# Graph attention, two layers: the first superchunk of layer 1 is gathered before the last rows of its table are there

## The chip, the cores and the metric

The kernel runs on one core of one Trainium2 chip. The metric is the device time of one execution in microseconds (us). The engines are PE (matmul, with PEld for its weight loads), DVE (vector), ACT (scalar), POOL (here the engine that issues the gathers) and SP (which issues nearly all other DMAs). Each has an instruction queue of its own that it works off in order; between queues only semaphores hold an order.

## The reference

Two graph attention layers over 6250 nodes with 256 features and 200,000 edges that are sorted by destination; layer 0 has four heads, layer 1 has one. Cut to one layer:

```python
hx = (x @ Wg).reshape(n, h, f)
te = relu(edge_attr @ We + be) * exp(x @ Wo + bo)[src][:, None]
s2, d2, ea2 = _add_self_loops(src, dst, te, n)   # a loop has the mean of its node's te
he = (ea2 @ Wge).reshape(-1, h, f)
al = leaky_relu((hx * a_s).sum(-1)[s2] + (hx * a_d).sum(-1)[d2] + (he * a_e).sum(-1), 0.2)
al = softmax of al over the edges of each destination
out = segment_sum(hx[s2] * al[:, :, None], d2) + b
```

Ahead of it stand a layer norm and a relu; layer 0's output goes through a relu with its residual and is layer 1's input. For each edge the row `hx[src]` is needed, with a few numbers that hang on the same node. Layer 1's row of a node can be computed only when layer 0 has finished that node.

## The kernel before, in words

**Tiles.** The edges are cut into columns of 128 edges, and the columns into superchunks of C = 24 (3072 edges). There are 66 superchunks a layer (`NS`): 64 with 24 columns, then one with 14 and one with 13. Step k counts superchunks over both layers: k = 0 to 65 are layer 0, 66 to 131 are layer 1. Since edges are sorted by destination, a superchunk holds all edges of some 95 neighbouring nodes, its window, which starts at node `base[s]` and is at most M = 112 nodes long.

**Tables.** `T[0]` and `T[1]` lie in device memory, one row of 268 or 260 floats for each node: the node's `hx`, its parts of the logit, and the exponential for its edges. `gather` issues one indirect DMA for each column on POOL; it fetches 128 rows of `T[l]` by the source indices `src` into `G`, one of three buffers (`gp[k % 3]`) of 128 x 24 x 270 floats.

**A superchunk's steps.** `spread`, `parts`, `blocks` bring the destination's part of the logit to the edges (DVE, a little PE). `rphase1` and `rphase2` compute the edge part (PE, ACT), `adst` adds the destination's part on PE, `edge_rows` transposes the result (DVE), `onehots` makes S, the matrices that say which of the window's nodes each edge belongs to. `logits`, `ends`, `links`, `maxima` need G: logits, running maxima per node, and the exponentials. `scale` multiplies G with them (on DVE in layer 0, on ACT in layer 1), `carried` adds what the superchunk before left of a shared node, `sums` multiplies S with G on PE and adds all columns in PSUM, `evict` copies the sums out.

**Finishing nodes.** `finish` merges a window's sums with its self loops and makes the node's new features. In layer 0 three row steps follow. `rows1` transposes the features (PE, then ACT), `rows2` multiplies them with layer 1's weights (PE), `rows3` adds the bias into a staging row (`t1row`, two buffers by the superchunk's parity), takes an exponential on ACT and stores it with three DMAs on SP: to `T[1]`, to the window copies `nd` (two arrays), and one number to the neighbouring window. In layer 1 only `rows3` does something: it stores the output.

**The order.** It is written out by hand: the program's text is the order of each engine's queue, and the framework adds the semaphore waits, for device memory too. `edges` loops over the superchunks, gathers one ahead, and finishes a window one or two steps later. The last three superchunks of a layer, called a, b, c (k = 63, 64, 65 and again 129, 130, 131), are interleaved by hand in `ending`, with `pv` and `late` the two before them (62 and 61). `after` is the first superchunk of layer 1 (k = 66), or None in the second layer. At the end of `ending` stood the gather of `after`, behind the last `rows3`, then its other steps up to `onehots`. The loop then goes on with the gather of 67.

`flag` and `general` are a slow way for inputs that fit no window; `checks` adds up what would call for it.

Of the kernel before, what the change touches and what calls it, by code (L numbers as in the profile page):

```python
# [22 lines left out]
F32 = mybir.dt.float32  # L23
# [8 lines left out]
P = 128  # L32
# [47 lines left out]
class Kernel:  # L80
# [364 lines left out]
    def indices(self, wp):  # L445
# [82 lines left out]
        self.slink = cp.tile([1, NS], F32, name="slink")  # L528
        V.tensor_tensor(self.slink, sc0[0:1, 0, :], sc0[0:1, 2, :], op=OP.is_equal)
        self.direct = max(NS - 2, 0)  # L530
        yield

        qd31 = cp.tile([1, 4, NS], F32, name="qd31")
# [9 lines left out]
    def checks(self, qd31, low):  # L543

        cp, V, NS, N, base, ll = self.cp, self.nc.vector, self.NS, self.N, self.base_f, self.lastloc
        chk = cp.tile([1, 9, NS + 1], F32, name="chk")
        V.memset(chk, 0.0)
        V.tensor_scalar(chk[:, 0, :NS], ll[0:1, :], float(M - 1), None, op0=OP.is_gt)
        V.tensor_scalar(chk[:, 5:9, :NS], qd31, 31.0, None, op0=OP.is_gt)
        nb = cp.tile([1, NS + 1], F32, name="nb")  # L550
        V.tensor_copy(nb[:, :NS], base[0:1, :])
        yield
        V.memset(nb[:, NS:], float(N))
        V.tensor_sub(nb[:, :NS], nb[:, 1:], nb[:, :NS])
        V.tensor_scalar(chk[:, 1, :NS], nb[:, :NS], float(M), None, op0=OP.is_gt)
        V.tensor_scalar(chk[:, 2, :NS], nb[:, :NS], 1.0, None, op0=OP.is_lt)
        yield
        V.tensor_copy(chk[:, 3, :NS], low)
        if self.direct:
            V.tensor_scalar(chk[:, 4, :self.direct], base[0:1, :self.direct], float(N - M), None, op0=OP.is_gt)  # L560
        V.memset(self.bad[:, 0:1], 0.0)
        V.tensor_reduce(self.bad[0:1, 0:1], chk.rearrange("p a b -> p (a b)"), axis=AX.X, op=OP.add)
        yield
# [80 lines left out]
    def edges(self, ctx):  # L644
        nc = self.nc
        self.gp += [self.pool(f"gath{i}", 1, ctx) for i in range(1, 3)]
        self.sp = self.pool("onehot", 2, ctx)
        self.wp = self.pool("work", 2, ctx)
        self.np_ = self.pool("nodes", 2, ctx)
        self.xp = self.pool("index", 1, ctx)  # L650
        self.ps_y = self.pool("ps_y", 1, ctx, space=PSUM)
        self.ps_1 = self.pool("ps_1", 1, ctx, space=PSUM)
        self.ps_f = self.pool("ps_f", 1, ctx, space=PSUM)
        self.lf = self.ps_1.tile([P, 512], F32, name="lf")
        nc.vector.memset(self.lf[0:4, 0:1], -BIG)
# [12 lines left out]
        self.adst(steps[0])  # L668
        self.onehots(steps[0])
        drain(self.soon)  # L670
        self.edge_rows(steps[0])

        pv = late = None
        self.ahead, self.rest = 1, None
        for k, st in enumerate(steps):
            nx = steps[k + 1] if k + 1 < len(steps) else None
            if st["s"] + 2 >= self.NS:
                continue
            for q in steps[k + 1:k + 3]:
                if q["L"] is st["L"] and "tw" not in q:  # L680
                    self.nodes(q)
            self.load_lb(k + 2)
            left = 99
            if self.ahead < len(self.groups):
                left = self.groups[self.ahead][0] - 2 - (self.ahead + 2 >= len(self.groups)) - k
            if self.rest is None and left <= 2:
                gi = self.index_load(self.ahead, self.xp)
                self.rest = self.index_group(self.ahead, self.xp, gi)
            if st["s"] + 3 == self.NS:
                self.ending(st, *steps[k + 1:k + 3], pv, late, steps[k + 3] if k + 3 < len(steps) else None)  # L690
                pv = late = None
# [12 lines left out]
            self.load_fl(k + 1)  # L704
            self.blocks(nx)
            drain(self.maxima(st))
            drain(y)
            self.load_ea(k + 2)
            self.rphase2(nx)
            self.adst(nx)  # L710
            if "S" not in st:
                self.onehots(st)
            if st["rows"]:
                self.scale_rows(st)
            else:
                drain(self.scale(st))
            self.carried(st)
            self.sums(st)
            if late:
                self.rows3(late)  # L720
                late = None
            self.onehots(nx)
            if pv:
                drain(self.finish(pv))
            self.evict(st)
            if pv:
                self.rows1(pv)
                late = pv
            self.index_on(left)
            if k >= 6:  # L730
                next(self.late, None)
                next(self.late, None)
            self.edge_rows(nx)
            if st["s"] + 4 == self.NS:
                drain(self.finish(st))
            pv = st
        self.flag()
# [9 lines left out]
    def ending(self, a, b, c, pv, late, after):  # L747
# [42 lines left out]
        drain(self.maxima(b))  # L790
        self.evict(a)
        n = b["C"]
# [71 lines left out]

    def flag(self):
        nc = self.nc
# [8 lines left out]
    def gather(self, st):  # L875
        nc, L = self.nc, st["L"]
        st["G"] = G = self.G0 if st["k"] == 0 else self.gp[st["k"] % 3].tile([P, C, 270], F32, name="G")
        idx = self.src[:, st["o"]:st["o"] + st["C"]]
        last = st["C"] - 1
        for c in (range(0) if st["k"] == 0 and self.CX > last else (last, *range(last))):  # L880
            nc.gpsimd.indirect_dma_start(  # L881
                out=G[:, c, 0:L.TW], out_offset=None, in_=self.T[L.l][0:self.N, :],
                in_offset=bass.IndirectOffsetOnAxis(ap=idx[:, c:c + 1], axis=0))
# [109 lines left out]
    def spread(self, st):  # L993


        if "Q" in st:
            return
        V = self.nc.vector
        q = self.pair(st["k"]) or [st]
        if len(q) < 2 or q[0]["C"] != q[1]["C"]:  # L1000
            q = [st]
        i, n, s = len(q), 32 * st["C"], st["s"]
        lb = st["lb2"] if i > 1 else st["lb"].unsqueeze(1)
        Q = self.wp.tile([P, 2, P], BF, name="Q")
        V.tensor_tensor(lb[:, :, :n], lb[:, :, :n], self.k_part.unsqueeze(2).to_broadcast([P, i, n]), op=OP.is_equal)  # L1005
        V.tensor_tensor(Q[:, :i].rearrange("p i (k j) -> p (i k) j", j=32),
                        self.k_32.unsqueeze(1).to_broadcast([P, 4 * i, 32]),
                        self.qsel[:, s:s + i, :].rearrange("p i k -> p (i k)").unsqueeze(2)
                        .to_broadcast([P, 4 * i, 32]), op=OP.is_equal)
        for j, t in enumerate(q):  # L1010
            t["Q"] = Q[:, j, :]

    def onehots(self, st, c0=0, c1=C):
        nc, o = self.nc, st["o"]
# [557 lines left out]
```

## Time and profile before

| what | value |
|---|---|
| median of 3 runs | 4052.73 us (4050.89 to 4054.78) |
| the profiled execution | 4055.1 us, its span 4053.3 us |
| busy: PE, DVE, ACT, POOL | 65%, 60%, 28%, 74% of the span |
| mean granted PE clock | 0.779 of full speed |
| gathers on POOL | 3102 + 24 in the prologue |

Times in timelines are microseconds from the start of the span: start, duration, engine, line, operation, output and inputs, how many instructions were merged, and in brackets how long the engine sat idle before and what released it. "issue" means that nothing the profile shows was waited for. In a list of waits the columns are the total in us, the times, and the longest. In tables of windows each engine has its busy time and number of instructions, then come the granted clock of PE (1.00 is full speed), the busy share of the 16 DMA engines, and GB/s. A matmul in float32 is shown as two instructions, so 24 matmuls are x48. An engine with a q behind its name is that engine's DMA queue, or its sequencer.

### The profile page before, as it was taken

The numbers are of one execution on the slowest core, as the hardware profiler recorded it, in microseconds if no ns is written. First come the engines' busy times: TensorE is split into PE (matmuls) and PEld (weight loads), VectorE is DVE, ScalarE is ACT, GpSimd is POOL, SyncE is SP. The second block draws the span as 40 slices with busy tenths as digits, with TensorE's granted clock in tenths as the row PEclk, the third lists the DMA queues.
The fourth block names the chain that finished last, engine by engine and source line by source line (L and its number), as shares of the span: only waits on it lengthen the run. The fifth ranks groups of instructions, "written<-read, shape, count | busy, mean of one in ns | idle before, by whom it ended". The sixth has DMA issues, their size and how long they took to land.

```text
span 4053.3 us, 37237 instructions
## 1 busy us (share of the span) xinstructions
PE 2639.2 (65%) x9878; PEld 1719.8 (42%) x9878; DVE 2436.3 (60%) x6063; ACT 1117.1 (28%) x2670; POOL 2998.9 (74%) x3253
## 2 busy tenths in 40 slices
PE   8776766666666766766646656656656566566565
PEld 6454444444444444444433433434434334334343
DVE  7887877877877877877744434333344343343445
ACT  5211111111111111111123434434334344343341
POOL 5777777777777777777747777777777777777775
PEclk9888878888887888888777777777777777777777
DMA  7455555555555555555534455455445445445443
GB/s 246 135 158 143 150 155 144 150 154 146 149 154 149 147 152 151 146 151 153 138 108 134 136 143 142 131 142 141 134 139 141 135 138 144 132 138 143 134 136 96
DMA packets 239250, 583.15 MB, mean 144 GB/s; under 512 B 64235, under 2 KB 96401, under 8 KB 238971
## 3 DMA queue, kind: packets, MB, share of 16 engines
q0 software_dynamic: 150144, 422.75, 39.3%
q1 hardware_dynamic: 88477, 157.30, 12.1%
q8 instruction: 85, 1.39, 0.1%
q14 instruction: 128, 1.05, 0.1%
q10 hardware_dynamic: 416, 0.67, 0.1%
HBM read 542.72 MB, written 37.86 MB: 143 GB/s over the span
## 4 chain that ended last, share of the span: by engine, by line
POOL 33%; DVE 27%; issue 14%; ACT 9%; PE 9%; DMA 8%; DVEq 0%; SPq 0%; ACTq 0%; POOLq 0%
POOL G L881 33%; DVE G L1192 8%; DMA G<-T,src 7%; ACT G L1201 7%; PE y L981 4%; DVE S L1021 4%; PE u L1211 2%; DVE lb L1005 2%; PE ps L439 1%; DVE m L1140 1%; DVE rt L1070 1%; ACT R L982 1%; DVE al L1088 1%; DVE al L1086 1%; DVE fb L1101 1%
## 5 line engine op out<-in xcount | busy, mean ns | idle before, releaser
L881 POOL DMA_INDIRECT G<-T,src x3102 | 2946.7, 950 | 1003.3 <-issue 916.3
L1211 PE MATMUL u<-G,S 128*128 128x270 f32 (+1 forms) x6252 | 1569.1, 414 | 187.4 <-DVE G L1182 184.1
L1211 PEld LDWEIGHTS u<-G,S 128*128 128x128 f32 x6252 | 1279.1, 206 | 479.0 <-DVE G L1182 212.2
L1201 ACT ACTIVATE G<-G,kw 128x256 f32<-128x256 f32 x1512 | 609.0, 497 | 0.0
L982 ACT ACTIVATE R<-y,webd 128x1024 f32<-128x1024 f32 (+2 forms) x264 | 235.4, 892 | 1322.8 <-PE y L981 817.4
L1108 PE MATMUL lf<-ident,fb 128*36 128x128 f32 (+1 forms) x132 | 50.3, 381 | 821.3 <-DVE fb L1101 795.7
L1084 DVE TENSOR_TENSOR G<-rt,G 128x96 f32<-128x96 f32 (+1 forms) x132 | 30.3, 230 | 866.0 <-DMA G<-T,src 866.0
L1192 DVE TENSOR_TENSOR G<-G,kps 128x6144 f32<-128x6144 f32 (+3 forms) x77 | 440.9, 5734 | 0.0
L1021 DVE TENSOR_TENSOR S<-kps,loc 128x3072 f32<-128x3072 f32 x132 | 437.6, 3315 | 4.6
L981 PE MATMUL y<-ea,webd 64*128 64x256 f32 (+1 forms) x1056 | 393.7, 840 | 50.9 <-ACT R L982 50.9
L990 PE MATMUL zad<-R,wea 128*64 128x384 f32 (+1 forms) x1056 | 308.2, 726 | 158.5 <-ACT R L982 158.2
L1108 PEld LDWEIGHTS lf<-ident,fb 128*36 128x36 f32 (+1 forms) x132 | 15.8, 119 | 863.4 <-DVE fb L1101 837.0
L990 PEld LDWEIGHTS zad<-R,wea 128*64 128x64 f32 x1056 | 88.2, 189 | 428.3 <-ACT R L982 339.8
L1216 ACT ACTIVATE U<-u 128x270 f32<-128x270 f32 (+1 forms) x132 | 51.8, 393 | 631.0 <-PE u L1211 631.0
L1243 DVE SCALAR_TENSOR_TENSOR mg<-U,mw 128x1 f32<-128x1 f32 x66 | 14.5, 220 | 281.3 <-ACT mw L1241 281.3
L981 PEld LDWEIGHTS y<-ea,webd 64*128 64x128 f32 x1056 | 124.7, 289 | 123.7 <-ACT R L982 70.3
L1174 DVE SCALAR_TENSOR_TENSOR G<-U,kw,G 1x257 f32<-1x257 f32 x62 | 29.6, 478 | 185.1 <-ACT G L1201 185.1
L1070 DVE STREAM_TRANSPOSE rt<-zad 128x768 f32<-128x768 f32 (+1 forms) x130 | 126.1, 970 | 8.5 <-PE zad L1056 8.5
L1042 PE MATMUL zad<-a,Q 128*128 128x12 bf16 (+1 forms) x132 | 26.1, 197 | 156.6 <-DVE a L1037 156.2
L439 PE MATMUL fin<-wg,h1T 128*128 128x260 f32 x264 | 125.3, 623 | 3.7 <-ACT h1T L1306 3.7
L1005 DVE TENSOR_TENSOR lb<-lb,kps 128x1536 bf16<-128x1536 bf16 (+1 forms) x68 | 112.9, 1661 | 0.0
L1316 ACT ACTIVATE t1row<-t1row 128x1 f32<-128x1 f32 x66 | 13.4, 203 | 349.9 <-DVE t1row L443 349.9
(195 smaller groups left out, 2238.4 us busy)
## 6 DMA issues: line engine op xcount, KB each, us to landing
G<-T,src POOLq DMA_INDIRECT x3102, 2.8
ea<-in_ea_dram SPq DMA_DIRECT2D x64, 768.0 KB
lb<-locrow SPq DMA_DIRECT2D x64, 384.0 KB
nd<-t1row SPq DMA_DIRECT2D x66, 225.8 KB
tw<-nd SPq DMA_DIRECT2D x66, 225.8 KB
tw<-T SPq DMA_DIRECT2D x66, 117.2 KB
T<-t1row SPq DMA_DIRECT2D x66, 113.8 KB
tw<-in_x_dram SPq DMA_DIRECT2D x66, 112.0 KB
```

The lines of the kernel that those rows point to most:

```text
L439: self.nc.tensor.matmul(ps[:, :L.MW], hT[:, k, :], self.wg[L.l][:, k, :], start=(k == 0), stop=(k == 1))
L881: nc.gpsimd.indirect_dma_start(out=G[:, c, 0:L.TW], out_offset=None, in_=self.T[L.l][0:self.N, :], in_offset=bass.IndirectOffsetOnAxis(ap= ...
L981: nc.tensor.matmul(y[:, i, :n], self.webd[l][r, :], ea[r, w], start=True, stop=True)
L982: nc.scalar.activation(R[:, :, w], y[:, :, :n], AF.Relu, bias=self.be[l])
L990: nc.tensor.matmul(st["zad"][i * PH:(i + 1) * PH, o], self.wea[l][0], R[:, i, w], start=True, stop=False)
L1005: V.tensor_tensor(lb[:, :, :n], lb[:, :, :n], self.k_part.unsqueeze(2).to_broadcast([P, i, n]), op=OP.is_equal)
L1021: nc.vector.tensor_tensor(st["S"][:, c0:c1, :], self.k_iota.unsqueeze(1).to_broadcast(w), self.loc[:, o + c0:o + c1].unsqueeze(2).to_broad ...
L1070: V.transpose(rv[:, :32 * c].rearrange("p (b n) -> p b n", b=2), z.rearrange("p (b n) -> p b n", b=2)[:, :, :16 * c])
L1108: self.nc.tensor.transpose(self.lf[0:e.shape[1], 1:P + 1], e, self.ident)
L1192: nc.vector.tensor_tensor(v, v, pw[:, c0:c1, :].unsqueeze(3) .to_broadcast([P, c1 - c0, H, L.F]), op=OP.mult)
L1201: self.nc.scalar.activation(v, v, AF.Copy, scale=st["w"][:, c:c + 1])
L1211: nc.tensor.matmul(st["u"][:, :L.W], S[:, i, :], G[:, i, 0:L.W], start=(j == 0), stop=(j == c - 1))
```

## The change

**The gather of `after`** is issued between the last of a's sums and `evict(a)`, into a's own buffer `G` (no new buffer is taken), columns in order from 0. By then the table holds the rows of all nodes ahead of a's first, so rows of nodes from `base[NS - 3]` on are fetched as what stands there. The steps of the two windows before are put further up for that: `rows3(late)`, `rows1(pv)`, `rows2(pv)` and `rows3(pv)` are all issued ahead of the gather. This order holds in both layers' endings, as the function is the same.

**What is added in layer 0's step 4** (`lacking`): two DMAs put zeros into the table's last 256 rows (a row read early is multiplied with 0 later, so it must be finite), and a few DVE instructions make `known`, which is 1 for each edge of superchunk 66 whose source lies ahead of the first missing node and 0 otherwise, and `k_lack`, the node number of each of the last 256 rows, or -1 where the row isn't missing.

**The completion.** `sources` loads the 3072 source indices of 66 into all 128 partitions (1.57 MB), into c's buffer, once c's sums are done. After c's `rows3`, `lack_rows` loads the table's last 256 rows as two tiles, `select` makes two one-hot matrices (a missing node's row against 3072 edges; one lies in c's buffer beside the indices, the other in an S buffer), and `complete` does for each column two matmuls, one-hot times rows, and on DVE `G = G * known + product`. Its 24 columns go in three groups of 8, between `blocks`, `rphase2` and `adst`, and behind `edge_rows` and `onehots`. The products use three places in turn: the two halves of the PSUM tile `y`, and `fin`. On the reference's inputs the first missing node is 6048, and 95 of the 3072 edges have a missing source. A new check sends inputs whose first missing node is below 6250 - 256 to the general way.

```diff
@@ checks
+        if self.early:
+            V.tensor_scalar(chk[:, 4, NS:], base[0:1, NS - 3:NS - 2], float(N - 2 * P), None, op0=OP.is_lt)
@@ edges
+            if k == 4 and self.early:
+                self.lacking()
@@ ending
         drain(self.maxima(a))
+        self.rows3(late)
         drain(y)
         self.load_ea(k + 2)
         self.rphase2(b)
         self.adst(b)
+        self.rows1(pv)
         drain(self.scale(a))
         self.carried(a)
         n = a["C"]
+        self.rows2(pv)
         self.sums(a, (0, n // 3))
-        self.rows3(late)
+        self.rows3(pv)
         self.edge_rows(b)
...
-        self.rows1(pv)
         self.spread(c)
         self.parts(c)
         self.sums(a, (n // 3, n // 2))
         self.links(b)
         self.sums(a, (n // 2, n))
+        early = after and self.early
+        if early:
+            self.gather(after, a["G"])
         self.load_fl(k + 2)
-        self.rows2(pv)
         drain(self.maxima(b))
...
         self.adst(c)
-        self.rows3(pv)
         self.carried(b)
...
         self.sums(c, (1, m), (0, 1))
+        if early:
+            self.sources(after)
         f = self.finish(b)
...
         if after:
-            self.gather(after)
+            fill = iter(())
+            if early:
+                self.lack_rows(after)
+                self.select(after)
+                fill = self.complete(after)
+            else:
+                self.gather(after)
             self.nodes(after)
             self.spread(after)
             self.parts(after)
             self.blocks(after)
+            for _ in range(C // 3):
+                next(fill, None)
             self.rphase2(after)
             self.adst(after)
+            for _ in range(C // 3):
+                next(fill, None)
             self.edge_rows(after)
             self.onehots(after)
+            drain(fill)
@@ new functions
+    def lacking(self):
+        nc, cp, N, NS = self.nc, self.cp, self.N, self.NS
+        V, W = nc.vector, self.L[1].TW
+        none = self.a["x"][N:N + 2 * P, :].rearrange("n d -> (n d)")[0:P * W].rearrange("(p w) -> p w", w=W)
+        for n in (N - 2 * P, N - P):
+            nc.sync.dma_start(self.T[1][n:n + P, :], none)
+        first = self.base_f[:, NS - 3:NS - 2]
+        self.known = cp.tile([P, C], F32, name="known")
+        V.tensor_scalar(self.known, self.src[:, 0:C], first, None, op0=OP.is_lt)
...
+    def sources(self, st):
+        n = C * P
+        X = self.gp[2].tile([P, C, 270], F32, name="G").rearrange("p c d -> p (c d)")
+        st["row"] = r = X[:, 0:n].bitcast(I32)
+        self.nc.sync.dma_start(r, self.a["srow"].rearrange("c p -> (c p)").partition_broadcast(P))
+        st["sel"] = [self.sp.tile([P, C, P], F32, name="S").rearrange("p c e -> p (c e)"), X[:, n:2 * n]]
+
+    def select(self, st):
+        for j, t in enumerate(st["sel"]):
+            self.nc.vector.tensor_tensor(t, st["row"], self.k_lack[:, j:j + 1].to_broadcast([P, C * P]), op=OP.is_equal)
+
+    def lack_rows(self, st):
+        st["tail"] = [self.np_.tile([P, 272], F32, name="U", bufs=3) for _ in range(2)]
+        for j, t in enumerate(st["tail"]):
+            n = self.N - 2 * P + P * j
+            self.nc.sync.dma_start(t[:, :self.L[1].TW], self.T[1][n:n + P, :])
+
+    def complete(self, st):
+        nc, W, G = self.nc, self.L[1].TW, st["G"]
+        y = self.ps_y.tile([P, 2, 512], F32, name="y")
+        ps = (y[:, 0, :], y[:, 1, :], self.ps_f.tile([P, 512], F32, name="fin"))
+        for c in range(C):
+            q = ps[c % 3][:, :W]
+            for j in range(2):
+                nc.tensor.matmul(q, st["sel"][j][:, c * P:(c + 1) * P], st["tail"][j][:, :W], start=(j == 0), stop=(j == 1))
+            nc.vector.scalar_tensor_tensor(G[:, c, 0:W], G[:, c, 0:W], self.known[:, c:c + 1], q, op0=OP.mult, op1=OP.add)
+            yield
```

The places that the prediction's steps rest on, in the built programs. Names carry the number of their buffer where that matters. First POOL, from a's gather on; before:

```order
L881 DMA G_11770<-T0_60,src_149 128x268 x24
L881 DMA G_11973<-T0_60,src_149 128x268 x14
L881 DMA G_11988<-T0_60,src_149 128x268 x13
L881 DMA G_12381<-T1_61,src_149 128x260 x24
L881 DMA G_12436<-T1_61,src_149 128x260 x24
```

And now:

```order
L905 DMA G_11781<-T0_60,src_149 128x268 x24
L905 DMA G_11984<-T0_60,src_149 128x268 x14
L905 DMA G_11999<-T0_60,src_149 128x268 x13
L905 DMA G_11781<-T1_61,src_149 128x260 x24
L905 DMA G_12529<-T1_61,src_149 128x260 x24
```

The queue's order is the same; what moved is what 66's gather (the first from T1) waits for: it writes a's buffer, and each of its 24 DMAs waits for the matmul of a that reads the same column.

Then SP, from the last flag load to the loads of 66's windows (T is table 1, t1row the staging rows of a, b, c); now:

```order
L955 DMA fl<-flags 4x516 x2
L1060 DMA G<-in_srow_dram 128x3072
L1419 ISA
L1419 DMA T_61<-t1row_175 112x260
L1421 DMA nd_63<-t1row_175 112x516
...
L1419 DMA T_61<-t1row_175 112x260
L1421 DMA nd_63<-t1row_175 112x516
L962 TENSOR_LOAD base_i
L1424 ISA
L1424 DMA nd_62<-t1row_175 1x1
L1073 DMA U<-T_61 128x260 x2
L971 DMA tw_176<-nd_62 112x516
```

Before:

```order
L931 DMA fl<-flags 4x516 x2
L1345 ISA
L1345 DMA T_61<-t1row_175 112x260
L1347 DMA nd_63<-t1row_175 112x516
...
L1350 DMA nd_62<-t1row_175 1x1
L947 DMA tw_176<-nd_62 112x516
```

The index load now stands ahead of a's stores, and the two loads of the table's tail stand between c's stores and 66's window loads. In the built program a's store to T waits for the eight DMA lanes of the early gather.

Last, PE and DVE from layer 1's first part on. PE now, the first columns of the completion (each row is one matmul of a column's two):

```order
L1116 MATMUL zad<-a_12429,Q 128x3
L1083 MATMUL y<-U,S 128x260
L1083 MATMUL y<-U,G 128x260
L1083 MATMUL y<-U,S 128x260
L1083 MATMUL y<-U,G 128x260
L1083 MATMUL fin<-U,S 128x260
L1083 MATMUL fin<-U,G 128x260
```

Before the change the first row was followed by the matmuls `zad<-R` of `rphase2` at once. In the built program the third completion row, the first of y's second half, waits for DVE's add of the column before it: the two halves of y are one tile to the framework. DVE now, from c's last store on:

```order
L443 TENSOR_TENSOR t1row_175<-fin,bias_374 128x260
L1066 TENSOR_TENSOR S<-G,kps 128x3072
L1066 TENSOR_TENSOR G<-G,kps 128x3072
L1029 TENSOR_TENSOR lb<-lb,kps 128x1536
L1030 TENSOR_TENSOR Q<-kps,qsel 128x256
...
L1123 TENSOR_TENSOR aq_170<-zad,quad 128x4x3
L1084 TENSOR_SCALAR G<-G,known,y 128x260 x2
L1084 TENSOR_SCALAR G<-G,known,fin 128x260
```

The two selects stand ahead of `spread`, and the completion's adds (L1084) behind `blocks`; before, `spread` followed c's last row at once.

More of the change, by code (lines that the diff above doesn't have):

```diff
@@ L530, in indices @@
         self.direct = max(NS - 2, 0)
+        self.early = NS > 12
         yield
@@ L873, in flag, with gather @@
         nc.vector.tensor_scalar(self.flag_i, f[:, 0:1], 0.0, None, op0=OP.is_equal)
-    def gather(self, st):
+    def gather(self, st, G=None):
         nc, L = self.nc, st["L"]
-        st["G"] = G = self.G0 if st["k"] == 0 else self.gp[st["k"] % 3].tile([P, C, 270], F32, name="G")
+        own = G is not None
+        if not own:
+            G = self.G0 if st["k"] == 0 else self.gp[st["k"] % 3].tile([P, C, 270], F32, name="G")
+        st["G"] = G
         idx = self.src[:, st["o"]:st["o"] + st["C"]]
         last = st["C"] - 1
-        for c in (range(0) if st["k"] == 0 and self.CX > last else (last, *range(last))):
+        for c in range(0) if st["k"] == 0 and self.CX > last else range(last + 1) if own else (last, *range(last)):
             nc.gpsimd.indirect_dma_start(
@@ L1011, in spread @@
             t["Q"] = Q[:, j, :]
+    def lacking(self):
[7 more added lines that the diff above has]
+        V.tensor_scalar(self.known, self.src[:, 0:C], first, None, op0=OP.is_lt)
+        t = cp.tile([P, 2, 2], F32, name="lack")
+        for j in range(2):
+            V.tensor_scalar(t[:, 0, j:j + 1], self.iota_p, float(N - 2 * P + P * j), None, op0=OP.add)
+        V.tensor_scalar(t[:, 1, :], t[:, 0, :], first, None, op0=OP.is_ge)
+        V.scalar_tensor_tensor(t[:, 0, :], t[:, 0, :], 1.0, t[:, 1, :], op0=OP.add, op1=OP.mult)
+        self.k_lack = self.kps[:, P + 40:P + 42]
+        V.tensor_scalar(self.k_lack, t[:, 0, :], -1.0, None, op0=OP.add)
@@ new lines, in lack_rows @@
+    def lack_rows(self, st):
[9 more added lines that the diff above has]
+            q = ps[c % 3][:, :W]
+            for j in range(2):
+                nc.tensor.matmul(q, st["sel"][j][:, c * P:(c + 1) * P], st["tail"][j][:, :W], start=(j == 0), stop=(j == 1))
+            nc.vector.scalar_tensor_tensor(G[:, c, 0:W], G[:, c, 0:W], self.known[:, c:c + 1], q, op0=OP.mult, op1=OP.add)
+            yield
```

## The prediction

> **What bounds the kernel now.** I read the page's groups of instructions first, then POOL's waits, then the timelines of POOL, DVE, PE and SP around the gap between the layers. The group with most busy time is the row gather on POOL:
>
> ```profile
> L881 POOL DMA_INDIRECT G<-T,src x3102 | 2946.7, 950 | 1003.3 <-issue 916.3
> ```
>
> One gather takes 950 ns and is followed by 0.30 us of issue, 1.25 us in all; 3102 of them make 3878 of the 4053 us. What POOL waits for from the gap to the last gathers (the answer counts the one wait that ends at its start):
>
> ```profile
> POOL G L881 <- issue: 465.8, 1529, 0.3
> POOL G L881 <- DMA T<-t1row: 40.1, 1, 40.1
> POOL G L881 <- DVE ade L1073: 7.0, 23, 0.3
> ```
>
> Only 0.3 us gaps and one real wait. POOL's timeline at that wait, with the first gathers of superchunks 67 and 68:
>
> ```profile
> 2026.42 0.95 POOL L881 DMA_INDIRECT G<-T,src  x1 [0.30 <-issue]
> ...
> 2067.49 0.94 POOL L881 DMA_INDIRECT G<-T,src  x1 [40.12 <-DMA T<-t1row]
> ...
> 2097.45 0.95 POOL L881 DMA_INDIRECT G<-T,src  x1 [0.30 <-issue]
> ...
> 2127.44 0.95 POOL L881 DMA_INDIRECT G<-T,src  x1 [0.30 <-issue]
> ```
>
> So layer 1 is a chain of gathers, 30.0 us for each superchunk of 24. Superchunk 66 (layer 1's first) starts at 2067.49, 67 at 2097.45, 68 at 2127.44. The other engines wait for it:
>
> ```profile
> 2099.12 0.20 DVE L1084 TENSOR_TENSOR G<-rt,G 128x24 f32<-128x24 f32 x1 [19.59 <-DMA G<-T,src]
> ...
> 2129.10 0.20 DVE L1084 TENSOR_TENSOR G<-rt,G 128x24 f32<-128x24 f32 x1 [17.88 <-DMA G<-T,src]
> ```
>
> Whatever shifts the gathers of 68 and later shifts the end by as much. The sum therefore asks for one time: when the gather of 68 starts.
>
> **The early gather.** Its 24 gathers leave the stretch after 2067.49 for POOL's 40.12 us of idle time. It writes the buffer of superchunk 63 (a), each column once a's matmul has read it:
>
> ```profile
> 2024.15 5.74 PE L1211 MATMUL u<-G,S 128*128 128x270 f32 x24
> ...
> L1345 SPq EVENT_SEMAPHORE  x66: 17/28/156, 180.8 to 2060.6; - x66
> ```
>
> (In a line's summary the numbers are the least, median and longest ns.) PE ends those at 2029.9 and stays ahead of POOL, which is free at 2026.42 + 1.25 = 2027.7. The table rows it needs (superchunk 62) are stored before, since their steps now stand ahead of a's sums. Each early gather has two waits, so a semaphore instruction more; SP's takes 28 ns, 24 of them 0.7 us. Last gather ends: 2027.7 + 30.0 + 0.7 - 0.3 = 2058.1. Landing: the last one before 2097.45 ended at 2097.15 and DVE started at 2099.12, so 2.0 us: 2060.1.
>
> **The new wait on SP.** The store of a's rows into the table now waits until the early gather has read it. Behind it on SP stand the stores of b and c (64, 65), the tail loads and the node loads. Before:
>
> ```profile
> 2055.54 0.33 SPq L1345 DMA_DIRECT2D T<-t1row  x1
> 2055.91 0.43 SPq L1347 DMA_DIRECT2D nd<-t1row  x1
> 2057.11 0.28 SPq L1350 DMA_DIRECT2D nd<-t1row  x1
> ...
> 2064.47 0.32 SPq L1345 DMA_DIRECT2D T<-t1row  x1
> ...
> 2067.30 1.28 SPq L947 DMA_DIRECT2D tw<-nd  x3
> ...
> 2069.99 0.16 DVE L1034 CAST a<-tw 128x1 bf16<-128x1 f32 x1 [3.79 <-DMA tw<-nd]
> ```
>
> From c's store to the gather it releases is 2067.49 - 2064.47 = 3.0 us; each store waits for the one ahead. Thus a's goes at 2060.2 (4.7 later than before), b's at 2063.2, c's at 2066.2, and 67 is gathered from 2069.2 to 2099.2, 28.2 us earlier than before. That would be the whole gain, were it not for what follows. The moved row steps of 61 and 62 only change places ahead of c's logits; I count nothing, as the sum goes through the early gather and the store of a; uncovered they are one 0.43 us add and two matmuls.
>
> **What 68 waits for.** The second half of the one-hot matrices and the indices lie in the buffer that 68 is gathered into, so 68 waits for the last completion matmul. Until then on DVE, with today's rows:
>
> ```profile
> 2059.83 0.42 DVE L1296 TENSOR_TENSOR t1row<-tw,hw 128x256 f32<-128x256 f32 x1
> ...
> 2063.78 0.43 DVE L443 TENSOR_TENSOR t1row<-fin,bias 128x260 f32<-128x260 f32 x1 [2.96 <-PE fin L439]
> 2064.12 1.74 DVE L1005 TENSOR_TENSOR lb<-lb,kps 128x1536 bf16<-128x1536 bf16 x1
> 2065.78 0.42 DVE L1006 TENSOR_TENSOR Q<-kps,qsel 128x256 bf16<-128x256 f32 x1
> ...
> 2074.83 0.98 DVE L1070 STREAM_TRANSPOSE rt<-zad 128x768 f32<-128x768 f32 x1 [3.67 <-PE zad L1056]
> 2075.85 0.23 DVE L1073 TENSOR_REDUCE ade<-rt 128x24 f32<-128x72 f32 x1
> ...
> 2076.18 3.36 DVE L1021 TENSOR_TENSOR S<-kps,loc 128x3072 f32<-128x3072 f32 x1
> ...
> L1326 DVE SCALAR_TENSOR_TENSOR fb<-tw,mw,fb x66: 467/485/498, 2149.5 to 4041.0; 128x256 f32<-128x256 f32 x66
> ```
>
> c writes the staging row that a's stores read, so L1296 waits for a's second store (2060.6 + 2.5) and the add at L443 for the third (2061.8 + 2.2 = 2064.0): DVE is at 2064.5. Two selects, same size as L1021: 6.7 us, 2071.2. The two rows of spread: 2073.3. The node load goes out at about 2071.0, when c's stores have landed, and is there 2.7 us later, 2073.7. The parts (0.75) and their matmul: PE starts completing at 2074.8.
>
> A column is two 128x260 matmuls, the shape of L439, in two granted clocks, and the logit matmuls in between:
>
> ```profile
> 2029.72 1.04 PE L439 MATMUL fin<-wg,h1T 128*128 128x260 f32 x4
> ...
> 2061.64 2.10 PE L439 MATMUL fin<-wg,h1T 128*128 128x260 f32 x4 [0.53 <-ACT h1T L1306]
> ...
> 2071.21 2.83 PE L990 MATMUL zad<-R,wea 128*64 128x384 f32 x8 [0.27 <-DVE aq L1049]
> 2073.97 0.82 PE L1056 MATMUL zad<-lb,aq 128*128 128x384 bf16 x2
> ...
> 2109.77 10.72 PE L1211 MATMUL u<-G,S 128*128 128x261 f32 x48
> ```
>
> Back to back at full clock it is 10.72 / 12 = 0.89 us, at half clock twice that, 1.75. Both y halves are one buffer to the program: the second waits until DVE has added the first, 0.15 of drain and 0.5 of add (row L1326), while fin overlaps. Three columns: 3 x 0.89 + 0.7 = 3.4 us, at half clock 6.0. The clock (PE alone: busy, granted clock, DMA share, GB/s):
>
> ```profile
> 2058.00:2100.00 42.00, 6.53 (x17) 0.51 0.44 122
> 2100.00:2109.50 9.50, 6.93 (x20) 0.50 0.57 174
> 2109.50:2122.00 12.50, 11.00 (x50) 0.99 0.49 139
> ```
>
> It is 0.5 when the completion starts, and rises only in a dense burst. I take the first three columns at half clock, the rest at full: 6.0; columns 3 to 7, 3.4 + 2.5; logit matmuls, half of 2.83 + 0.82, 1.8; columns 8 to 15, 8.6; 16 and 17, 2.5. That is 2099.6. Meanwhile DVE does L1070, L1073 and L1021 (4.8 us) after column 15's add, so column 18's buffer is free only at 2103.1; 18 to 23 take 6.8: 2109.9. If the 3.5 us pause drops the clock, 2.5 more. I take 2111.
>
> The Trainium skill (TensorE: Matmul & The Clock Gate, Part 1) speaks against the change here: it says that the array idles at half clock, is released after about 3.4 us of sustained work, and falls back after an idle window of like length. This trace agrees on the two levels (0.50, 0.99); by that rule alone the cold part would be 3.4 us, an estimate from the page that gives 2109, and the pause would sit on the edge of a fall back.
>
> **The sum.** 68 is gathered from 2111.0 instead of 2127.4: 16.4 us less. DVE's logits of 66 come at 2111.5 instead of 2099.12; a's buffer is next wanted at 2141, and 66's sums (L1211, 2120.5 before, 21.4 after the logits) end at 2133, so POOL stays the bound. The writes at step 4 and the extra check hide under POOL, which waits nowhere there; without cover, five DVE instructions of some 0.2 us. The profiled execution took 4055.1 (span 4053.3), 2.4 above the median 4052.7: 4038.7 on its scale, 4036.3 on the median's. I predict 4036.
>
> **The index load.** 1.57 MB for 128 partitions goes on SP when c's sums end:
>
> ```profile
> 2044.22 6.16 PE L1211 MATMUL u<-G,S 128*128 128x270 f32 x26 [1.02 <-ACT R L982]
> ...
> 2107.00:2112.00 5.00, 5.00 (x21) 2.78 (x18) 1.38 (x3) 5.00 (x14) 3.78 (x5) 0.73 0.92 317
> 2112.00:2120.00 8.00, 8.00 (x38) 6.87 (x37) 0.00 (x0) 3.97 (x10) 5.87 (x8) 1.00 0.39 107
> ...
> 2150.50:2157.50 7.00, 3.11 (x15) 2.32 (x13) 0.66 (x2) 0.39 (x1) 5.17 (x7) 1.00 0.69 167
> ```
>
> Beside gathers (107 GB/s), the load of ea gets 317 - 107 = 210 GB/s, that of lb only 60. By ea's pace it takes 7.5 us and lands at about 2060, before a's store; by lb's 26 us, 2077. It copies one row to 128 partitions, ea's count and not lb's four rows, so I take ea's. The Trainium skill (DMA: Bandwidth & Descriptors, Rules for kernel authors) says that an outermost dimension under 16 confines a DMA to so many engines; lb's slow row agrees, and by it this load would run at ea's pace.
>
> **The rivals.**
> 1. The index load goes at lb's pace and the stores queue behind it. Selects from 2077 end at 2083.5, PE starts at 2087, 68 at 2123: 4049. For it: one source read many times, as lb's. Against: the outer count.
> 2. PE stays at half clock in the completion (2100 to 2109.5 shows 73% busy without a rise): 8 x 6.0 + 3.7 + a pause of 3.5 from 2074.8 is 2130, 4055. It ends slower where the columns also run singly, at L439's isolated 2.10 plus 0.65: 24 x 2.75 + 3.7 + 4.8 = 74.5, 68 at 2149, 22 late: 4074. It decides where a column costs over (2127.4 - 2074.8 - 7) / 24 = 1.9 us.
> 3. The completion is hidden: 68 starts at 2099.2, all 28.2 gained, 4024.5. It would need 0.9 us a column with no DVE between.
> 4. The change does nothing, since its check falls to the general path: no, the first missing node is 6048 on this input, above the limit 6250 - 256.
>
> **How the numbers follow.** Forecast (68 between 2103 and 2119) 0.74; hidden or nearly 0.07; slow index load 0.07; half clock 0.12, of which 0.05 stays within 0.2%. A run tells 0.2%, 8 us, from no change. Faster 0.81, same 0.12, slower 0.07. The range goes from rival 3's neighbourhood, 4027, to past rival 1, 4051; the forecast's own is 4028 to 4045.
>
> **What would show it.** 24 gathers inside the old idle time, from 2027.7; SP's store of a right after them; 67 from about 2069; a POOL wait of about 12 us before 68, released by the completion matmuls on PE; PE clock 0.5 at their start. Wrong if the stores queue behind the index load, if a column takes nearer 2 us than 1.15, or if DVE and not POOL paces superchunks 67 to 70.

## The result and the profile after

The changed kernel takes 4036.85 us (median of 7 runs, 4035.22 to 4041.07); the kernel before took 4052.73 (7 runs, 4049.7 to 4055.17) beside it. The ratio is 0.996 (95% interval 0.9951 to 0.997): 15.9 us faster, where 4036 was forecast. The profiled execution took 4041.07 (span 4039.3), 4.2 above its median; POOL is 1.8 us later in it than in the trace of before from layer 0's prologue on (the last gather of c starts at 2028.21 instead of 2026.42), so times after the gap are compared less 1.8.

POOL's waits in the changed kernel (total, times, longest), and its timeline at the early gather's first and last column and the first columns of 67 and 68:

```profile
POOL G L905 <- issue: 912.4, 2993, 1.0
POOL G L905 <- PE fin L1083: 16.2, 1, 16.2
POOL G L905 <- DMA T<-t1row: 9.3, 1, 9.3
```

```profile
2028.21 0.95 POOL L905 DMA_INDIRECT G<-T,src  x1 [0.30 <-issue]
2029.46 0.95 POOL L905 DMA_INDIRECT G<-T,src  x1 [0.30 <-PE u L1285]
...
2058.85 0.94 POOL L905 DMA_INDIRECT G<-T,src  x1 [0.30 <-issue]
...
2069.10 0.94 POOL L905 DMA_INDIRECT G<-T,src  x1 [9.31 <-DMA T<-t1row]
...
2115.06 0.94 POOL L905 DMA_INDIRECT G<-T,src  x1 [16.25 <-PE fin L1083]
```

The idle 40.1 us are filled with 24 gathers; 9.3 us of waiting for c's store are left, and a new wait of 16.2 us stands before 68, released by the completion's last product. Superchunk 68 starts 12.4 us earlier than before (2127.44), or 14.2 less the 1.8. After it POOL waits nowhere until its last gather, as before. From the end of c's last gather to the first one behind c's store it is 39.9 us, against 40.1 before.

SP's stores, DVE around the selects, and PE's completion at its start, at the pause and at its end:

```profile
2061.82 0.33 SPq L1419 DMA_DIRECT2D T<-t1row  x1
...
2063.88 0.32 SPq L1419 DMA_DIRECT2D T<-t1row  x1
...
2066.39 0.32 SPq L1419 DMA_DIRECT2D T<-t1row  x1
```

```profile
2064.84 0.42 DVE L1370 TENSOR_TENSOR t1row<-tw,hw 128x256 f32<-128x256 f32 x1 [3.44 <-DMA nd<-t1row]
...
2066.04 3.35 DVE L1066 TENSOR_TENSOR S<-G,kps 128x3072 f32<-128x3072 int32 x1
2069.30 3.35 DVE L1066 TENSOR_TENSOR G<-G,kps 128x3072 f32<-128x3072 int32 x1
```

```profile
2075.37 1.22 PE L1083 MATMUL y<-U,S 128*128 128x260 f32 x2
2076.38 1.08 PE L1083 MATMUL y<-U,G 128*128 128x260 f32 x2
2078.03 1.24 PE L1083 MATMUL y<-U,S 128*128 128x260 f32 x2 [0.58 <-DVE G L1084]
...
2088.73 1.51 PE L1014 MATMUL zad<-R,wea 128*64 128x384 f32 x8
...
2104.96 1.23 PE L1083 MATMUL y<-U,S 128*128 128x260 f32 x2 [2.99 <-DVE G L1084]
...
2114.18 0.60 PE L1083 MATMUL fin<-U,G 128*128 128x260 f32 x2
```

PE's busy time, granted clock, DMA share and GB/s over the completion, by stretch:

```profile
2074.00:2084.00 10.00, 7.68 (x17) 0.51 0.61 159
2084.00:2102.00 18.00, 15.48 (x66) 1.00 0.36 98
...
2104.00:2106.00 2.00, 1.04 (x3) 0.55 0.00 0
2106.00:2110.00 4.00, 3.42 (x9) 0.50 0.00 0
2110.00:2112.00 2.00, 2.00 (x8) 0.75 0.00 0
```

The completion lasts from 2075.4 to 2114.8, in two stretches at half clock: its first four columns, and the three after DVE's pause.

### The profile page after: what moved, and what is told of

Its sections match the earlier page's. It is cut to its first block, busy times and chain, and to the rows that moved or that the text cites. A ratio compares the mean times of both kernels' runs of the same rounds, so it can differ in the third digit from the quotient of the medians.

```text
span 4039.3 us, 37506 instructions
## 1 busy us (share of the span) xinstructions
PE 2658.8 (66%) x9974; PEld 1744.1 (43%) x9974; DVE 2454.5 (61%) x6096; ACT 1117.3 (28%) x2670; POOL 2998.3 (74%) x3253
## 3 DMA queue, kind: packets, MB, share of 16 engines
q0 software_dynamic: 150144, 422.75, 39.2%
## 4 chain that ended last, share of the span: by engine, by line
POOL 32%; DVE 26%; issue 14%; PE 10%; ACT 10%; DMA 8%; DVEq 0%; SPq 0%; ACTq 0%; POOLq 0%
POOL G L905 32%; ACT G L1275 8%; DVE G L1266 7%; DMA G<-T,src 7%; PE y L1005 4%; DVE S L1095 3%; PE u L1285 3%; DVE lb L1029 2%; PE ps L439 1%; DVE m L1214 1%; DVE rt L1144 1%; ACT R L1006 1%; DVE al L1162 1%; DVE al L1160 1%; DVE fb L1175 1%
## 5 line engine op out<-in xcount | busy, mean ns | idle before, releaser
L1014 PE MATMUL zad<-R,wea 128*64 128x384 f32 (+1 forms) x1056 | 295.2, 699 | 158.2 <-ACT R L1006 158.2
L1014 PEld LDWEIGHTS zad<-R,wea 128*64 128x64 f32 x1056 | 85.2, 182 | 414.3 <-ACT R L1006 334.7
L1390 ACT ACTIVATE t1row<-t1row 128x1 f32<-128x1 f32 x66 | 13.4, 203 | 354.0 <-DVE t1row L443 354.0
```

Of the source, the lines that this page charges most:

```text
L1014: nc.tensor.matmul(st["zad"][i * PH:(i + 1) * PH, o], self.wea[l][0], R[:, i, w], start=True, stop=False)
```

## Experiments

Theory A is the prediction's: POOL's gathers set the pace, and what the early gather wins is cut by 68's wait for the completion's last matmul. Rival B: the moved row steps give the gain. Rival C: the completion is hidden, and its end is not what 68 waits for.

The twelve kernels ran in three groups, each beside the kernel before, on three chips. There the kernel before took 4780.07, 4877.77 and 4054.83 us, so only the third group is on a chip like the prediction's. The first two answer another question, which comes after. Each chip was used in one group only: what is put down to the chip could also lie in the occasion.

### A chip where the kernel before takes 4055: half of the sums

These four leave out every second column of the sums, so that PE's part could be told apart wherever they ran (the main lines; the numbers that they compute are not the reference's):

```diff
@@ sums
             for i in range(a, b):
+                if i % 2:
+                    continue
...
@@ merge
-            V.scalar_tensor_tensor(ze, U[:, L.p:L.p + H], w[:, 0, :H], w[:, 1, :H], op0=OP.mult, op1=OP.add)
+            V.scalar_tensor_tensor(ze, U[:, L.p:L.p + H], w[:, 0, :H], w[:, 1, :H], op0=OP.add, op1=OP.add)
...
```

**The kernel before with half the sums.** 

> The kernel before with every second column left out of the sums of every superchunk (24 of 48 matmuls; the denominators add instead of multiplying, so that nothing divides by zero; the numbers are not the reference's). All gathers are made. It asks what paces the program on a chip where the kernel before takes 4780 to 4880. If it is PE, whose last 10 sums of 48 stand 2 to 3 us apart there: the stalls shrink with the number of instructions to some half, and the time falls to between 4053 and 4450. If it falls all the way to 4053, POOL's gathers set the pace again. If something else paces that chip: as the kernel before, within 1%. On a chip where the kernel before takes 4053: 4053, unchanged, since POOL never waits there.

Measured: 4047.06 (4044.62 to 4049.24, 11 runs), 0.9981 of the kernel before (0.9972 to 0.999). With 1562 matmuls (3124 of the profile's instructions) fewer the time falls by 8 us, where none was expected. So PE's sums are not the pace here, but they are not free: in the trace, POOL's wait of 4.8 us early in layer 0, which ACT releases, is gone, and the one at the gap is 37.4 us instead of 40.1.

**The changed kernel with half the sums.** 

> The changed kernel with the same half of the sums left out, to be set against the kernel before with half of them. Theory A, with POOL as the pace: 16 us less than that, where the completion takes the 39 us of the changed kernel's first trace (2075.4 to 2114.8); with a stall of 13 us in the completion, as in the trace of 4894 us (from 2504.9 to 2518.0), 68 starts as late as before and the two are equal within 5 us. If PE still sets the pace: 10 to 28 us more.

Measured: 4033.39 (4032.01 to 4037.93, 5 runs): 13.7 less than the kernel before with half the sums, near theory A's 16.

**The early gather without the completion.**

```diff
-        if early:
-            self.sources(after)
...
             if early:
-                self.lack_rows(after)
-                self.select(after)
-                fill = self.complete(after)
+                pass
```

> The early gather without the completion (the 95 edges with missing rows are summed with wrong rows), half of the sums left out. Theory A with POOL as the pace: superchunk 67 is gathered 28 us earlier and 68 straight after it, so 28 us less than the kernel before with half the sums, and 12 to 28 less than the changed one. If PE sets the pace: 0 to 10 us less than before, since an earlier gather alone makes nothing on PE earlier but the first sums.

Measured: 4019.54 (4018.31 to 4022.59, 5 runs): 27.5 less, forecast 28. The completion thus costs 13.9 us of the 27.5 (C said none).

**The completion kept, but 68's buffer not hung on it.**

```diff
@@ ending
-            for _ in range(C // 3):
-                next(fill, None)
+            drain(fill)
             self.edge_rows(after)
             self.onehots(after)
-            drain(fill)
@@ sources
-        st["sel"] = [self.sp.tile([P, C, P], F32, name="S").rearrange("p c e -> p (c e)"), X[:, n:2 * n]]
+        st["sel"] = [self.sp.tile([P, C, P], F32, name="S").rearrange("p c e -> p (c e)") for _ in range(2)]
```

> The changed kernel with both selection matrices in buffers of S and edge_rows and the one-hot matrices of 68 after the completion, half of the sums left out. The completion's matmuls are all there, only the buffer of 68 does not hang on them. Theory A with POOL as the pace: 68 follows 67 without a wait for the matmuls, and with 12 sums the buffer for 69 comes free in time: 20 to 28 us less than the kernel before with half the sums, as the one without the completion. Rival C (the completion's end is not what 68 waits for): as the changed kernel with half the sums. If PE sets the pace: as that one too.

Measured: 4021.55 (4020.84 to 4023.47, 5 runs): 25.5 less than before with half the sums, 11.8 less than the changed one, with all products made. The edit does two things, since the first part also takes DVE's pause out of the completion: from 67's first gather to the last product it is now 39.2 us instead of 43.4. What tells A from C is the trace: 68 starts with no wait, 9.2 us before the last product ends, where in the changed kernel it was released by that product. POOL at 68 in the kernel before, the changed one, the one without completion and the last (there also at 69, and PE's last products), each with half the sums:

```profile
2120.62 0.94 POOL L881 DMA_INDIRECT G<-T,src  x1 [0.30 <-issue]
```

```profile
2107.73 0.95 POOL L905 DMA_INDIRECT G<-T,src  x1 [13.94 <-PE fin L1083]
```

```profile
2092.68 0.94 POOL L901 DMA_INDIRECT G<-T,src  x1 [0.30 <-issue]
```

```profile
2091.52 0.95 POOL L903 DMA_INDIRECT G<-T,src  x1 [0.30 <-PE y L1081]
...
2124.09 0.95 POOL L903 DMA_INDIRECT G<-T,src  x1 [2.86 <-ACT U L1290]
```

```profile
2099.69 1.04 PE L1081 MATMUL fin<-U,S 128*128 128x260 f32 x4
```

68 starts 12.9, 27.9 and 29.1 us earlier than in the first; the times fall by 13.7, 27.5 and 25.5. The last gives 2.9 back at 69, whose buffer waits for 66's sums, which start only after the completion; with all the sums some 6 us were estimated (run on the chip at 4878, below), and that was not run on such a chip. B was not run alone here either. Against it speaks that the gap from c's last gather to the first one behind c's store kept its length (39.9 against 40.1 us in the two traces with all sums): what changed in it is that 24 gathers stand inside.

### Two chips where the kernel before takes 4780 and 4878

**Only the moved row steps** (chip at 4780): `self.early = NS > 12` becomes `self.early = False`. 

> The row steps keep their new places, but the early gather, the zeros, the index load and the completion are left out; superchunk 66 is gathered at the end of the ending as before the change. Theory A (the gain is the 24 gathers that move into POOL's idle time, less what the completion costs): as the kernel before, 4052.7 us, within 0.1%, and POOL's wait of 40 us stays. Rival B (the moved row steps shorten the ending): about 4037.

Measured: 4785.78 (4777.52 to 4792.62, 11 runs), 1.0012 (1.0003 to 1.0021): no gain from the order alone.

**No completion** (the edit shown above, all sums; both chips). 

> The completion, its index load, its selects and its tail loads are left out (95 of 3072 edges of superchunk 66 keep the rows that stood there), the early gather stays. Theory A (superchunk 68 waits on POOL for the completion's last matmul, and that wait is on the path): 68 starts when 67's gathers are issued, at 2069.1 + 30.0 = 2099.1 instead of 2115.1, 16 us less than the changed kernel: 4021. Rival C (the completion is covered, something else in 66 or 67 sets the pace): 4034 to 4040.

> The early gather without the completion (no missing-row matrices, no selects, no completion matmuls; the sums over the 95 edges whose rows were missing are wrong). Theory A: 68 is gathered straight after 67, at about 2099 instead of 2115, so 16 us less than the changed kernel: 4021 where that takes 4037. Rival B (the moved row steps give the gain): as the changed kernel, 4037. Rival C (the completion is hidden): 4037 as well. If the matmuls pace the program: 0.999 of before, as it was there, and 28 us below the changed kernel.

Measured: 4776.86, 0.999 (0.9981 to 0.9999) and 4871.87, 0.9991 (0.9977 to 1.0005). Where 27.5 us were won above with half the sums, 3.2 and 5.9 are won here, and the second is not clear of the noise. On the chip at 4780 neither branch of the expectation fits, as both took POOL for the pace; on the other the branch in which the matmuls set it (0.999) does.

**The changed kernel itself** (chip at 4878). 

> The changed kernel itself, on the chip of these runs. Theory A (POOL's gathers set the pace of layer 1, and superchunk 68 is gathered when the completion's last matmul is done): 0.996 of the kernel before wherever the gathers pace the program, 4037 where the kernel before takes 4053. If the matmuls pace the program, as on a chip where the kernel before takes 4780 and single matmuls stand 2 us apart, the early gather only fills time of POOL that is idle anyway, and the completion adds 24 x 1.15 us = 28 us to the PE, the engine that is waited for: 1.000 to 1.006 there (4780 to 4808).

Measured: 4898.47 (4894.27 to 4903.17, 5 runs), 1.0049 (1.0033 to 1.0065): 20.7 us slower than before, and 26.6 slower than without the completion. On this chip the change loses, as the expectation had it for a chip on which the matmuls set the pace (1.000 to 1.006).

**Two PSUM tiles in turn** (chip at 4780): `ps = (y[:, 0, :], fin)` and `ps[c % 2]`. 

> The products alternate between one half of y and fin, so no column waits for the add of the column right before it. Theory A: the 8 waits of 0.58 us go, 4.6 us, perhaps 1 more as the denser PE leaves the half clock sooner: 4031 to 4033. Rival C: 4037.

**edge_rows and onehots after the completion** (chip at 4780): the edit of `ending` shown with the last kernel above, alone. 

> All 24 columns are completed before edge_rows and onehots of superchunk 66. Theory A: PE's pause of 3.0 us before column 18 goes, and with it the second stretch at half clock (some 3.4 us): 68 starts 6.4 us earlier, 4030.5; DVE's 4.8 us then stand behind the last add and cost nothing, since POOL sets the pace. If only the pause counts and the clock stays up or down regardless: 4034. Rival C, or if DVE's logits of 66 set the pace: 4037.

Measured: 4794.6, 1.0024 (1.0014 to 1.0033), and 4795.68, 1.003 (1.0017 to 1.0042). Both expectations were made for POOL as the pace and say nothing here; the changed kernel was not run on that chip, so what the two edits do by themselves stays open.

**Both selection matrices in S, all sums** (chip at 4878; `edge_rows` and `onehots` stand behind the completion here too, the edit is the last one above). 

> Both selection matrices lie in buffers of S, so that the buffer of 68 is held only by the index row, whose last reader is the second select (2072.6 in the changed kernel). Theory A: 68 follows 67 with no wait for the matmuls, at about 2099; but 66's logits still come after the completion (2110 to 2115), its sums end at 2135, and the buffer of 63 and 66 is wanted again for 69 at 2129: 69 waits some 6 us. 16 - 6 = 10 us less than the changed kernel, 4027; between 4021 (no wait at 69) and 4033. Rival C (the completion's end is not what 68 waits for): 4037, with the wait before 68 as long as it was. If the matmuls pace the program: as the changed kernel there, within 0.1%.

Measured: 4909.53, 1.007 (1.0051 to 1.0089).

**PE kept busy ahead of the completion** (chip at 4878): 32 matmuls of `ident` with itself into `y`, between `lack_rows` and `select`. 

> 32 matmuls of the identity on itself ahead of the completion, into its own psum buffer, while PE waits for the selects. The first three and a half columns ran at half clock, 8.3 us where full clock gives some 3.5. Theory A: the completion ends 4 us earlier, 68 starts 4 us earlier, 4033 where the changed kernel takes 4037. If the 32 matmuls end too early and the clock has fallen back before the first column: 4037. Rival C: 4037. If the matmuls pace the program: as the changed kernel there.

Measured: 4905.87, 1.0061 (1.0043 to 1.008). Neither gains: they lie 11.1 and 7.4 us above the changed kernel's median there, where both were expected as that kernel if the matmuls set the pace. Their intervals overlap with its 1.0049, but all four runs with the busy PE are above all five of the changed kernel. In the first, 68 no longer waits, but 69 then waits 54.8 us for a matmul.

**What sets the pace there.** POOL's waits in the changed kernel on the chip at 4878:

```profile
POOL G L905 <- PE zad L1116: 399.7, 62, 7.4
POOL G L905 <- PE fin L1378: 216.9, 36, 10.4
POOL G L905 <- PE u L1285: 117.5, 22, 11.3
POOL G L905 <- DMA T<-t1row: 41.4, 1, 41.4
...
POOL G L905 <- PE fin L1083: 30.7, 1, 30.7
```

734 us of waiting for PE in the three rows ahead of the completion's, where the trace of 4041 us has one long wait, of 16. And PE has many waits whose end the profile puts down to nothing ("issue"). Its sums of one superchunk in that trace, and POOL's last gather of a burst and first of the next:

```profile
2919.69 8.30 PE L1285 MATMUL u<-G,S 128*128 128x261 f32 x37
2931.05 0.38 PE L1285 MATMUL u<-G,S 128*128 128x261 f32 x1 [3.05 <-issue]
2933.90 0.59 PE L1285 MATMUL u<-G,S 128*128 128x261 f32 x1 [2.47 <-issue]
...
2944.39 3.24 PE L1285 MATMUL u<-G,S 128*128 128x261 f32 x6 [2.20 <-issue]
```

```profile
2940.00 0.95 POOL L905 DMA_INDIRECT G<-T,src  x1 [0.30 <-issue]
2947.90 0.95 POOL L905 DMA_INDIRECT G<-T,src  x1 [6.95 <-PE zad L1116]
```

After 37 dense instructions the next come one by one, 2 to 3 us apart, until 3.4 us after the end of the burst's last gather. ACT's and DVE's steps for these columns had ended by 2926. In the completion PE stood still for 13 us, and went on when the gathers of 67 were over (PE, then DVE's adds, then POOL's last gather):

```profile
2504.37 0.60 PE L1083 MATMUL y<-U,G 128*128 128x260 f32 x2
2517.95 1.24 PE L1083 MATMUL y<-U,S 128*128 128x260 f32 x2 [12.97 <-issue]
```

```profile
2509.01 0.48 DVE L1084 SCALAR_TENSOR_TENSOR G<-G,known,fin 128x260 f32<-128x260 f32 x1 [5.23 <-remote]
2517.41 0.48 DVE L1084 SCALAR_TENSOR_TENSOR G<-G,known,y 128x260 f32<-128x260 f32 x1 [7.91 <-remote]
```

```profile
2516.47 0.95 POOL L905 DMA_INDIRECT G<-T,src  x1 [0.30 <-issue]
```

"remote" is a release that the profile can put down to no instruction. PE's "issue" is misleading here: its matmul writes y's second half and starts 0.06 us after DVE's second add has ended, as at the other columns, where the profile names that add. So PE waited for DVE, and DVE's adds came late, though the products that they add had been made by 2505.

The clearest pair is the gap itself, on the chip at 4780. The row steps alone (POOL idle there), and the early gather without completion, at the same place in PE's queue, c's edge part; for the second also ACT:

```profile
2386.16 0.54 PE L1005 MATMUL y<-ea,webd 64*128 64x160 f32 x4
2387.39 0.70 PE L1005 MATMUL y<-ea,webd 64*128 64x256 f32 x4 [0.69 <-ACT R L1006]
```

```profile
2389.75 0.54 PE L1001 MATMUL y<-ea,webd 64*128 64x160 f32 x4
2406.76 1.23 PE L1001 MATMUL y<-ea,webd 64*128 64x256 f32 x4 [16.47 <-issue]
```

```profile
2396.32 0.40 ACT L1286 ACTIVATE U<-u 128x270 f32<-128x270 f32 x1 [10.46 <-issue]
2406.18 0.53 ACT L1002 ACTIVATE R<-y,webd 128x320 f32<-128x320 f32 x1 [9.33 <-remote]
```

With gathers beside it PE stands 16.5 us at a place where it otherwise stands 0.7. In both kernels it goes on 0.05 us after ACT's step on the matmul before: here ACT's step came 15.9 us after that matmul, without gathers at once. So again it isn't PE alone that is late; whether ACT is, or the signal that y is there, the profile doesn't tell. Over the whole trace of 4894 us, waits put down to "issue" or "remote" make 1478 us on PE, 810 on ACT and 798 on DVE, in that of 4041 us 0, 0 and 0.2. Some of them are plain waits whose releaser the profile lost: 1.21 us ahead of PE's L1014 are "issue" in the first and put down to ACT's R in the second. POOL in the same two kernels, at the first gather behind c's store, in the second also at the first early one:

```profile
2424.21 0.94 POOL L905 DMA_INDIRECT G<-T,src  x1 [58.48 <-DMA T<-t1row]
```

```profile
2380.04 0.94 POOL L901 DMA_INDIRECT G<-T,src  x1 [10.67 <-PE u L1281]
...
2451.19 0.94 POOL L901 DMA_INDIRECT G<-T,src  x1 [41.44 <-DMA T<-t1row]
```

From c's last gather to the first one behind c's store it is 58.5 us without early gathers, and with them 2451.19 - 2380.04 + 10.67 = 81.8: the gap has grown by 23.3, of which the pause is 15.8. Of the 30 us of gathers, 30 - 23.3 = 6.7 are won; the medians of the two kernels differ by 8.9. Add a completion of 24 columns on PE and DVE, which are late there, and the change costs time. Why the steps of PE, ACT and DVE come late beside gathers on these two chips and not on the other is not settled: no run changed the gathers' rate or PE's instruction count there (the kernels with half the sums ran on another chip).

## Why the prediction was right, and where its terms were off

- **What bounds the kernel** held on that chip: what 68 gains shows in the time (the kernels with half the sums: 12.9, 27.9, 29.1 against 13.7, 27.5, 25.5, where the last is 26.6 at 69).
- **The early gather** and **the new wait on SP** held: its 24 gathers end at 2059.8, a's store goes 2.0 us later, as forecast. From a's store to 67's first gather it was 7.3 us instead of 9.0: the stores followed each other in 2.1 and 2.5 us, not 3.0.
- **The index load** was quick: from 2052 to 2058 it and the gathers moved 313 to 400 GB/s, from 2058 to 2060 129, and a's store left 2.0 us behind the last early gather, as forecast without this load. Rival 1 falls.

```profile
2052.00:2054.00 2.00, 0.97 (x2) 0.84 (x3) 1.83 (x8) 0.97 (x3) 1.40 (x2) 0.75 0.92 320
2054.00:2056.00 2.00, 2.00 (x5) 0.84 (x5) 1.82 (x8) 0.62 (x2) 1.70 (x2) 0.50 0.99 400
2056.00:2058.00 2.00, 1.20 (x6) 0.20 (x2) 0.84 (x6) 1.12 (x2) 1.39 (x3) 0.90 0.80 313
```

- **What 68 waits for** was named rightly and is shown by the kernel with both matrices in S. DVE's wait for the stores (3.44 at L1370) and the selects (6.6) came as written. The start was 2075.4, or 2073.6 less layer 0's 1.8, and so 1.2 ahead of the forecast 2074.8: the node load, which the forecast had as the last to come, was there when DVE was done with `spread`. The mis-sized term is the half clock. Four columns ran cold, not three: the first eight took 13.4 us (forecast 11.9). Columns 8 to 17 with the logit matmuls took 13.2 (12.9). The pause was 3.0 instead of 3.5, but it did drop the clock, and the last six columns took 9.8 (6.8, and half of 2.5 for the risk). Together the end came 3.8 later than 2111, or 2.0 without layer 0's shift: 3.2 lost in these stretches, 1.2 won at the start. Of the 0.65 us for a wait between the halves of y, no run shows the 0.15 as drain; the wait measured 0.58, 0.48 of it the add.
- **The sum** still met the time, since 14.2 us at 68 and 1.3 us of a shorter tail behind the last gather (29.3 instead of 30.6) make 15.5 of the 15.9. The forecast for 68 was 16.4, so 68 started 2.2 later than the sum had it, and the tail, which had no term in it, gave 1.3 of that back. That 4036 came out within 1 us is in this part luck.
- **Rivals 2 to 4**: the clock did rise in the completion (1.00 from 2084 to 2102), so 2 falls here; 3 is near what lifting the hold on 68's buffer gives, and not what the change is. Rival 4 falls with the gain itself.
- What the prediction did not have is that its premise doesn't hold on every chip: all its rows come from a trace in which PE, ACT and DVE are not late beside gathers. On the chip at 4878 the forecast's sign is wrong, and the ways it named for a loss (half clock, columns run singly) are not what makes it there.

## What to carry to other kernels

Price a transfer moved into idle time by what its landing place is held for afterwards: here half of 28 us went to a buffer that held a matrix until the last product, and with half the sums 11.8 of 13.9 came back when the matrix was put elsewhere and DVE's pause taken out. A stage that starts PE from idle and then waits some 3 us for a vector engine paid half clock twice here. And before moving work onto PE and DVE because they are idle, see on more than one chip whether they keep pace beside the DMAs.

## What the runs showed of the hardware

- A pause of 2.99 us was enough for the granted clock to fall from 1.00 to 0.55 and 0.50, and a stretch that kept PE busy at some 90% from 2075.4 on needed 8.3 us to be given the full clock; the stretch behind the pause needed 6.0. Earlier in the same trace a pause of 2.12 us (2050.90 to 2053.03) was followed by a fall to 0.50 as well (2054 to 2056, in the rows above). The Trainium skill (TensorE: Matmul & The Clock Gate, Part 1) gives about 3.4 us for both. Here the fall came sooner and the release later.
- The kernel before took 4053 to 4055, 4780 and 4878 us on different chips. Where it takes 4053 to 4055, gathers beside other work cost PE, ACT and DVE nothing that a trace shows. On the other two, PE's sums come 2 to 3 us apart until the gathers are done, PE stands 13 and 16.5 us until late steps of DVE and ACT are done, and POOL waits for PE. The gathers themselves (0.95 us, 0.30 between) are the same on all.
